# Layers 1 to 3 of a gated cross-attention decoder: the second token group's transposes and query products issued among the attention's leading tiles

## The chip, the cores and the metric

The kernel runs on one core of a Trainium2 chip. The metric is the device time of one execution in microseconds (us), median of the runs shown; a second number, the span, comes from a profiled execution and leaves out what lies before the first and after the last recorded instruction. The engines are named as in the profile: PE (TensorE matmul), PEld (its weight loads), DVE (VectorE), ACT (ScalarE), POOL (GpSimd), SP (SyncE, which issues most DMAs).

## What is computed

Four decoder layers act on a float32 stream x of 4 sequences of 256 tokens and 256 channels; the context has 64 tokens of 64 channels per sequence. Each layer adds a gated cross-attention and then a gated feed-forward part, each fed by a layer norm of x:

```python
x = x + tanh(g_xattn[0]) * L0_xattn(layernorm(x), ctx);  x = x + tanh(g_ffn[0]) * L0_ffn(layernorm(x))  # 16 experts, top 6
x = x + tanh(g_xattn[1]) * L1_xattn(layernorm(x), ctx);  x = x + tanh(g_ffn[1]) * L1_ffn(layernorm(x))  # ternary weights
x = x + tanh(g_xattn[2]) * L2_xattn(layernorm(x), ctx);  x = x + tanh(g_ffn[2]) * L2_ffn(layernorm(x))  # int8-like linear
x = x + tanh(g_xattn[3]) * L3_xattn(layernorm(x), ctx);  x = x + tanh(g_ffn[3]) * L3_ffn(layernorm(x))  # 8 experts, top 2
```

The attention of layer 1 has latent keys and values (16 heads of 128, folded by the kernel into weights that map x straight to a 64-wide latent query per head); those of layers 2 and 3 are plain 16-head attention with head size 16, a causal mask and a scale of 1/4:

```python
qp = q @ Wq.T;  k, v = split(latent_kv @ Wkv_expand.T)
attn = softmax(where(causal, q_h @ k_h.T / sqrt(16), lowest));  out = (attn @ v_h) @ Wout.T
```

## The kernel before

The 1024 tokens are 8 tiles of 128 (`NT`), in two groups of 4 tiles = 512 tokens (`NG`, `TH`). All of x stays in SBUF, one buffer per tile.

`layernorm(g)` (lines 374 to 398) takes the statistics of a group's four tiles on DVE (L379, L380), the square root on ACT (L382), and writes four normalised tiles `xn` on DVE (L394), or on ACT for layer 3 (L391). `transposed` (L400) turns them with 8 PE transposes (L406) into `xT`, through two PSUM tiles of the tag `mm` (4 buffers). `evacuate` (L128) copies out of PSUM, one call on ACT (L132) and the next on DVE (L134) in turn. `mm2` (L418, products at L421) makes one query product out of two matmuls over the 256 channels.

Each attention then goes over the 8 tiles in `in_flight` (L458): in round i it asks an optional generator `beside` for one step, makes the scores and exponentials of tile i, adds the output of tile i-3 to x (`gated_add`, L456), normalises the weights of tile i-1 (`weights`: sum L435 and reciprocal L436 on DVE, product L437 on POOL), and attends with tile i-2. Scores go into PSUM tiles `wide` (2 buffers). The row maximum and the subtraction are on DVE (layer 1: L427, L428; layers 2 and 3: L934, L936), the exponential on ACT (L429, L945). `attend` begins with 8 transposes of the weights (L451) and their two copies on ACT (L452); in layer 1 the products with the values follow (L656); in layers 2 and 3 the products L953, a copy on ACT (`ctxTok`, L962) and the output products (L965).

Ahead of the first tile of the attention, both groups' inputs are made:

- Layer 1 (`attention1`, L833): group 0's layer norm and transposes, its first 4 query products, group 1's layer norm and transposes, then the other 12 of the 16 query products (L842, 128 x 512 each), each copied by `evacuate` into the latent queries `qcT`. `latent_attend` (L610) also makes the values of a sequence (L623) every second tile, and its scores are L641.
- Layers 2 and 3 (`attention23`, L887): for both groups the layer norm, the transposes and two query products; then four scaled copies on ACT (L902) into separate tiles `qT`, which take the buffers of the tag `xT` (2 buffers). The scores are L923, with the mask added by L913 for every second tile.

In layer 2, `keyed` (L974) passes the making of layer 3's keys and values (`keys_values`: L860, L863, L875, L882) as `beside`, one step per round; layer 3 passes nothing.

A scheduler of the framework takes the program's order as a priority and decides the order in which each engine gets its instructions; on the chip each engine's queue is then followed in that order.

Of the kernel before, what the change touches and what calls it, by code (L numbers as in the profile page):

```python
# [16 lines left out]


# [1 line left out]

# [1 line left out]

# [6 lines left out]
F32 = mybir.dt.float32  # L29
# [8 lines left out]
P = 128  # L38
# [3 lines left out]
TH = 512  # L42
NG = T // TH
# [3 lines left out]
NP = NH // 2  # L47
# [34 lines left out]
def tile_flamingo(ctx: ExitStack, tc: tile.TileContext, a: dict, out: bass.AP):  # L82
    nc = tc.nc
# [316 lines left out]
    def transposed(tiles, dtype=F32):  # L400

        xT = sb.tile([P, 2, TH], dtype, tag="xT", name="xT", bufs=2)
        for c in range(2):
            ps = ps_mm()
            for i, n in enumerate(tiles):
                nc.tensor.transpose(ps[:, i * P : (i + 1) * P], n[:, c * P : (c + 1) * P], ident)  # L406
            evacuate(xT[:, c, :], ps)
        return xT
# [9 lines left out]
    def mm2(ps, w, xT):  # L418

        for c in range(2):  # L420
            nc.tensor.matmul(ps, w(c), xT[:, c, :], start=(c == 0), stop=(c == 1))  # L421
# [36 lines left out]
    def in_flight(scores, attend, gate, beside=iter(())):  # L458

        made, outs = {}, {}  # L460
        for i in range(NT + 3):
            next(beside, None)
            if i < NT:
                made[i] = scores(i)
            if i >= 3:
                gated_add(i - 3, outs.pop(i - 3)[:, :D], gate)
            if 1 <= i <= NT:
                weights(made[i - 1])
            if 2 <= i < NT + 2:
                outs[i - 2] = attend(i - 2, made.pop(i - 2))  # L470
# [136 lines left out]
        t = big[:, HALF:].rearrange("p (g r t) -> p g r t", g=NG, r=NP)  # L607
        return [t[:, g] for g in range(NG)]

    def latent_attend(qcT, wvo, gate, swapped=False):  # L610


        vos: dict = {}

        def values(b):

            v = region(("wqk", "weff")[b % 2], 2048, "vo").rearrange("p (q j o) -> p q j o", q=4, j=2)
            for r in range(2):
                pss = [ps_mm() for _ in range(2)]
                for a_ in range(2):  # L620
                    for j, ps in enumerate(pss):
                        rows = slice(j * DC, (j + 1) * DC)
                        nc.tensor.matmul(  # L623
                            ps[a_ * L : (a_ + 1) * L, :],
                            bd_k[rows, b, j * L : (j + 1) * L],
                            wvo[rows, 4 * r + a_ : 4 * r + a_ + 3 : 2, :],
                            start=True,
                            stop=True,
                        )
                for j, ps in enumerate(pss):  # L630
                    evacuate(v[:, 2 * r : 2 * r + 2, (1 - j) if swapped and b >= B // 2 else j, :], ps.rearrange("p (q o) -> p q o", q=2))
            vos[b] = v.rearrange("p q j o -> p (q j) o")

        def scores(t):
            g, i = divmod(t, TPG)
            if t % 2 == 0:
                values(t // 2)
            ps = ps_wide()
            for pr in range(NP):
                q, a_ = divmod(pr, 2)  # L640
                nc.tensor.matmul(  # L641
                    ps[:, q // 2, q % 2 * 256 : (q % 2 + 1) * 256].rearrange("p (j a l) -> p j a l", j=2, a=2)[:, :, a_, :],
                    qcT[g][:, pr, i * P : (i + 1) * P],
                    bd_k[:, t // 2, :],
                    start=True,
                    stop=True,
                )
            e = t4([P, NH, L], "attn")
            exponentials(e, ps.rearrange("p a (h l) -> p (a h) l", l=L))
            return e  # L650

        def attend(t, e):
            aT, vo = transposed_pairs(e), vos[t // 2]
            ps = ps_mm()
            for s in range(NP):
                nc.tensor.matmul(ps[:, :D], aT[:, s, :], vo[:, s, :], start=(s == 0), stop=(s == NP - 1))  # L656
            return ps

        in_flight(scores, attend, gate)

    def attention0(gate):

# [170 lines left out]
    def attention1(gate):  # L833
        weff, wvo = kept.pop("fold1")
        qcT = latents()
        xT = [transposed(layernorm(0))]
        for g in range(NG):
            for pr in range(NP):
                if g == 0 and pr == NP // 2:
                    xT.append(transposed(layernorm(1)))  # L840
                ps = ps_mm()
                mm2(ps, lambda c: weff[:, c, pr * P : (pr + 1) * P], xT[g])  # L842
                evacuate(qcT[g][:, pr, :], ps)
        latent_attend(qcT, wvo, gate)


    def keys_values(layer, kbd, vbd):
# [39 lines left out]
    def attention23(layer, gate, beside):  # L887
        kbd, vbd = kept.pop(layer)
        w = loaded[f"L{layer}"]
        w_q = w[:, :512].rearrange("p (c o) -> p c o", c=2)  # L890
        w_o = w[:, 512:1024].rearrange("p (c o) -> p c o", c=2)
        products, qT = [], []
        for g in range(NG):
            xT = transposed(layernorm(g, layer == 3))
            pss = [ps_mm() for _ in range(2)]
            for half, ps in enumerate(pss):
                mm2(ps, lambda c: w_q[:, c, half * P : (half + 1) * P], xT)
            products.append(pss)
        for pss in products:
            q = sb.tile([P, 2, TH], F32, tag="xT", name="qT", bufs=2)  # L900
            for half, ps in enumerate(pss):
                nc.scalar.mul(q[:, half, :], ps, 0.25)  # L902
            qT.append(q)

        def scores(t):


            g, i = divmod(t, TPG)
            ps = ps_wide()
            masked = t % 2 == 0  # L910
            if masked:
                for a in range(2):
                    nc.tensor.matmul(  # L913
                        ps[:, a, :].rearrange("p (h l) -> p h l", l=L),
                        ident16,
                        causal16.unsqueeze(1).to_broadcast([P, 8, L]),
                        start=True,
                        stop=False,
                    )
            for half in range(2):  # L920
                for a in range(2):
                    rows = slice(a * L, (a + 1) * L)
                    nc.tensor.matmul(  # L923
                        ps[:, a, half * D : (half + 1) * D],
                        qT[g][rows, half, i * P : (i + 1) * P],
                        kbd[rows, half, t // 2].rearrange("p i l -> p (i l)"),
                        start=not masked,
                        stop=(half == 1 or not masked),
                    )

            e = t4([P, NH, L], "attn")
            src = ps.rearrange("p a (h l) -> p (a h) l", l=L)
            mx = small([P, NH], "mx")
            nc.vector.tensor_reduce(mx, src, AX.X, ALU.max)  # L934
            for a in range(2):
                nc.vector.tensor_tensor(  # L936
                    e.rearrange("p (f a i) l -> p a f i l", f=2, a=2)[:, a],
                    ps[:, a, :].rearrange("p (f i l) -> p f i l", f=2, l=L),
                    mx[:, a * 8 : (a + 1) * 8]
                    .rearrange("p (f i) -> p f i", f=2)  # L940
                    .unsqueeze(3)
                    .to_broadcast([P, 2, 4, L]),
                    ALU.subtract,
                )
            nc.scalar.activation(e, e, AF.Exp)  # L945
            return e

        def attend(t, e):
            aT = transposed_pairs(e)
            ps = ps_mm()  # L950
            for pr in range(NP):
                half, r = divmod(pr, 4)
                nc.tensor.matmul(  # L953
                    ps[r * 32 : (r + 1) * 32, half * P : (half + 1) * P],
                    vbd[:, t // 2, pr].rearrange("p j d -> p (j d)"),
                    aT[:, pr, :],
                    start=True,
                    stop=True,
                    tile_position=(0, r * 32),
                )  # L960
            cT = sb.tile([P, 2 * P], F32, tag="xn", name="ctxTok", bufs=6)
            nc.scalar.copy(cT, ps[:, : 2 * P])  # L962
            ps = ps_mm()
            for half in range(2):
                nc.tensor.matmul(  # L965
                    ps[:, :D], cT[:, half * P : (half + 1) * P], w_o[:, half, :], start=(half == 0), stop=(half == 1)
                )
            return ps

        in_flight(scores, attend, gate, beside)  # L970
        if layer == 3:
            used("L3")

# [826 lines left out]
```

## Time and profile before

| | |
|---|---|
| runs, us | 954.0, 962.89, 962.95; median 962.89 |
| the profiled execution | 967.09 us, span 965.3 us, mean granted PE clock 0.941 |
| busy of the span | PE 856.9 us (89%), PEld 555.5, DVE 509.9 (53%), POOL 345.7, ACT 286.8 |
| attention of layer 1, from group 0's first transpose | 478.9 us to about 575 us of the span |
| attention of layer 2, from group 0's first transpose | 637.3 us to about 705 us |
| attention of layer 3, from group 0's first transpose | 723.9 us to about 782 us |

How to read it: times are us from the start of the span. In the timeline a row has start, duration, engine, line, operation, written and read tiles with shapes, how many instructions were merged, and in brackets the idle time of the engine just before and what ended it. In the tables of stretches each engine has its busy time and count of instructions, PEclk is the clock that PE was granted, as a share of full speed, and then DMA share and rate. A 128 x 512 float32 product of one weight block stands as two rows of PE, so that the two matmuls of a query product are four rows.

### The profile page before, as it was taken

What the parts mean: (1) busy time and instruction counts of PE and PEld (TensorE: products, weight loads), DVE (VectorE), ACT (ScalarE), POOL (GpSimd) and SP (SyncE); (2) the same over time, 40 slices, a digit from 0 to 9 for tenths busy, and PEclk for the clock granted to TensorE, in tenths of its full rate; (3) what the DMA queues carried; (4) which work ended last, traced back from release to release, by engine and by line L of the source; (5) the groups of instructions that cost most, each with busy time, mean ns of one, the idle gap of its engine ahead of it and who ended that gap; (6) DMA issues with size and microseconds to landing.
All of it is one profiled execution on the core that took longest, in us unless ns stands there. A gap on an engine that the chain in (4) does not pass through costs nothing.

```text
span 965.3 us, 12724 instructions
## 1 busy us (share of the span) xinstructions
PE 856.9 (89%) x4467; PEld 555.5 (58%) x4467; DVE 509.9 (53%) x1299; ACT 286.8 (30%) x559; POOL 345.7 (36%) x262
## 2 busy tenths in 40 slices
PE   6999999999999999986199986997867889999994
PEld 4444336876667876764046872754544556666662
DVE  4566648748624444571427755867776856222220
ACT  2122014433112322322113445415534441122221
POOL 1454543110146787786001323402311302144421
PEclk9999999999779999998599999986988999999998
DMA  9201157000256666655640000360000012122223
GB/s 364 79 21 34 61 160 200 22 22 9 84 129 158 125 141 150 121 82 63 186 174 1 1 1 0 111 227 1 1 22 1 1 44 54 43 45 45 39 23 66
DMA packets 38762, 75.15 MB, mean 78 GB/s; under 512 B 6240, under 2 KB 26706, under 8 KB 37322
## 3 DMA queue, kind: packets, MB, share of 16 engines
q1 hardware_dynamic: 23562, 52.01, 16.0%
q0 software_dynamic: 14496, 20.47, 13.1%
q10 hardware_dynamic: 640, 1.84, 0.5%
q8 instruction: 39, 0.64, 0.3%
q14 instruction: 25, 0.20, 0.1%
HBM read 58.73 MB, written 16.61 MB: 78 GB/s over the span
## 4 chain that ended last, share of the span: by engine, by line
PE 31%; DVE 10%; issue 4%; ACT 3%; POOL 2%; DMA 0%; POOLq 0%; ACTq 0%; DVEq 0%
PE wide L1226 7%; PE mm L421 5%; PE mm L1250 3%; PE wide L1436 2%; PE mm L451 2%; PE mm L656 2%; PE mm L965 2%; PE wide L923 1%; PE mm L1457 1%; DVE mx L934 1%; DVE attn L936 1%; PE mm L1637 1%; PE mm L1241 1%; DVE big L1483 1%; POOL h L1482 1%
## 5 line engine op out<-in xcount | busy, mean ns | idle before, releaser
L437 POOL TENSOR_TENSOR attn<-attn,sm 128x1024 f32<-128x1024 f32 x32 | 60.9, 1903 | 212.5 <-DVE sm L436 192.5
L1235 DVE SCALAR_TENSOR_TENSOR blk<-wide,weight,blk 128x176 f32<-128x176 f32 (+1 forms) x75 | 37.0, 493 | 135.3 <-ACT blk L1234 121.2
L1262 POOL DMA_INDIRECT sums<-ring,big x55 | 88.1, 1601 | 33.6 <-issue 10.2
L421 PE MATMUL wide<-xT,big 128*128 128x512 f32 x192 | 86.7, 600 | 0.3 <-ACT big L556 0.3
L683 DVE TENSOR_TENSOR rope<-wide,big 128x512 f32<-128x512 f32 x96 | 59.6, 683 | 47.7 <-PE wide L421 46.6
L1174 POOL DMA_INDIRECT xs<-xd,big x55 | 54.9, 999 | 63.3 <-DMA sums<-x 35.6
L1215 PE MATMUL wide<-big,blk 128*128 x220 | 77.1, 472 | 0.0
L1226 PE MATMUL wide<-big,blk 128*128 x160 | 72.2, 593 | 0.5 <-DVE blk L1187 0.5
L1234 ACT ACTIVATE blk<-wide 128x176 f32<-128x176 f32 (+1 forms) x75 | 29.4, 392 | 122.3 <-PE wide L1226 60.2
L421 PEld LDWEIGHTS wide<-xT,big 128*128 128x128 f32 x192 | 35.0, 190 | 46.7 <-issue 40.5
L656 PE MATMUL mm<-vo,attnT 128*128 128x256 f32 x256 | 59.5, 386 | 0.9 <-ACT attnT L452 0.9
L1250 PE MATMUL mm<-big,blk 88*128 x220 | 57.4, 383 | 0.6 <-ACT blk L1243 0.5
L406 PE MATMUL mm<-ident,xn 128*128 128x128 f32 x112 | 19.4, 320 | 41.6 <-DVE xn L394 35.5
L656 PEld LDWEIGHTS mm<-vo,attnT 128*128 128x128 f32 x256 | 48.0, 193 | 9.1 <-ACT attnT L452 3.1
L456 DVE SCALAR_TENSOR_TENSOR x<-mm,tg,x 128x256 f32<-128x256 f32 x48 | 22.9, 478 | 54.9 <-PE mm L656 17.3
L1250 PEld LDWEIGHTS mm<-big,blk 88*128 88x128 f32 x220 | 41.9, 192 | 16.5 <-ACT blk L1243 1.5
L452 ACT COPY attnT<-mm 128x512 f32<-128x512 f32 x64 | 35.0, 588 | 54.6 <-PE mm L451 54.3
L1215 PEld LDWEIGHTS wide<-big,blk 128*128 128x128 f32 x220 | 40.6, 196 | 13.2 <-issue 1.3
L451 PE MATMUL mm<-ident,attn 128*128 128x128 f32 x256 | 38.0, 297 | 9.9 <-POOL attn L437 9.9
L435 DVE TENSOR_REDUCE sm<-attn 128x16 f32<-128x1024 f32 x32 | 38.8, 1212 | 14.9 <-ACT attn L429 12.4
L1174 POOL DMA_INDIRECT xs<-xd,scratch x20 | 19.5, 976 | 74.6 <-PE mm L1186 53.9
L1262 POOL DMA_INDIRECT sums<-ring,scratch x20 | 31.5, 1573 | 39.3 <-ACT ring L1261 16.8
(321 smaller groups left out, 1698.6 us busy)
## 6 DMA issues: line engine op xcount, KB each, us to landing
big<-in_L_w_gate_up SPq DMA_DIRECT2D x8, 1024.0 KB
big<-in_L_w SPq DMA_DIRECT2D x4, 1408.0 KB
big<-in_L_w_down SPq DMA_DIRECT2D x8, 512.0 KB
w_L_qk<-in_L_qk SPq DMA_DIRECT2D x4, 896.0 KB
big<-in_L_w SPq DMA_DIRECT2D x4, 704.0 KB
big<-in_L_wo SPq DMA_DIRECT2D x1, 2048.0 KB
xd<-xn SPq DMA_DIRECT2D x16, 128.0 KB
sums<-x SPq DMA_DIRECT2D x16, 128.0 KB
```

What stands on the lines that cost most here:

```text
L421: nc.tensor.matmul(ps, w(c), xT[:, c, :], start=(c == 0), stop=(c == 1))
L435: nc.vector.tensor_reduce(sm, e, AX.X, ALU.add)
L437: nc.gpsimd.tensor_tensor(e, e, sm.unsqueeze(2).to_broadcast([P, groups, n]), ALU.mult)
L451: nc.tensor.transpose(ps[:, i * P : (i + 1) * P], ev[:, pr * P : (pr + 1) * P], ident)
L656: nc.tensor.matmul(ps[:, :D], aT[:, s, :], vo[:, s, :], start=(s == 0), stop=(s == NP - 1))
L683: nc.vector.tensor_tensor(m[:, s, :].rearrange("q (b t) -> q b t", t=S), ps[:, s, :].rearrange("q (b t) -> q b t", t=S), table, ALU.mult,)
L1174: nc.gpsimd.indirect_dma_start(out=xs, out_offset=None, in_=self.xd, in_offset=bass.IndirectOffsetOnAxis(ap=self.gather[:, b : b + 1].bitc ...
L1215: nc.tensor.matmul(ps[:, 0, : 2 * n], st[:, c * P : (c + 1) * P], self.w[:, bass.ds(r + c * 2 * n, 2 * n)], start=False, stop=(c == 1),)
L1226: nc.tensor.matmul(ps[:, k, :n], st[:, c * P : (c + 1) * P], self.w[:, bass.ds(r + (2 * c + k) * n, n)], start=(c == 0), stop=(c == 1),)
L1235: nc.vector.scalar_tensor_tensor(s, lin, self.weight.pop(b), s, ALU.mult, ALU.mult)
L1250: nc.tensor.matmul(ps[:, :D], hT[:, j * P : (j + 1) * P], self.w[: self.chunk, bass.ds(r + j * D, D)], start=(j == 0), stop=(j == self.n - 1),
L1262: nc.gpsimd.indirect_dma_start(out=self.sums[b % len(self.sums)], out_offset=bass.IndirectOffsetOnAxis(ap=self.scatter[:, b : b + 1].bitca ...
```

## The change

In layers 1 to 3 only group 0's layer norm, transposes and queries are made ahead of the attention. Those of group 1 become a generator, `queries(1)`, that `in_flight` steps through by `beside`: in round 0 its layer norm; in layer 1 the transposes and 4 query products in round 1 and 4 more in round 2; in layers 2 and 3 the transposes in round 1 and the two products with their scaled copies in round 2. The scores of group 1 begin with tile 4. In layer 2 the generator for layer 3's keys and values is stepped along with it. In layers 2 and 3 the queries are written over the inputs `xT` in place of tiles of their own. `latent_attend` gets the parameter `beside`, and hands it on.

```diff
-    def latent_attend(qcT, wvo, gate, swapped=False):
+    def latent_attend(qcT, wvo, gate, swapped=False, beside=iter(())):
...
-        in_flight(scores, attend, gate)
+        in_flight(scores, attend, gate, beside)
...
     def attention1(gate):
         weff, wvo = kept.pop("fold1")
         qcT = latents()
-        xT = [transposed(layernorm(0))]
-        for g in range(NG):
+        def queries(g):
+
+            xn = layernorm(g)
+            yield
+            xT = transposed(xn)
             for pr in range(NP):
-                if g == 0 and pr == NP // 2:
-                    xT.append(transposed(layernorm(1)))
                 ps = ps_mm()
-                mm2(ps, lambda c: weff[:, c, pr * P : (pr + 1) * P], xT[g])
+                mm2(ps, lambda c: weff[:, c, pr * P : (pr + 1) * P], xT)
                 evacuate(qcT[g][:, pr, :], ps)
-        latent_attend(qcT, wvo, gate)
+                if pr % 4 == 3:
+                    yield
+
+        for _ in queries(0):
+            pass
+        latent_attend(qcT, wvo, gate, beside=queries(1))
...
     def attention23(layer, gate, beside):
...
-        products, qT = [], []
-        for g in range(NG):
-            xT = transposed(layernorm(g, layer == 3))
+        qT = []
+
+        def queries(g):
+
+            xn = layernorm(g, layer == 3)
+            yield
+            xT = transposed(xn)
+            yield
             pss = [ps_mm() for _ in range(2)]
             for half, ps in enumerate(pss):
                 mm2(ps, lambda c: w_q[:, c, half * P : (half + 1) * P], xT)
-            products.append(pss)
-        for pss in products:
-            q = sb.tile([P, 2, TH], F32, tag="xT", name="qT", bufs=2)
             for half, ps in enumerate(pss):
-                nc.scalar.mul(q[:, half, :], ps, 0.25)
-            qT.append(q)
+                nc.scalar.mul(xT[:, half, :], ps, 0.25)
+            qT.append(xT)
+
+        for _ in queries(0):
+            pass
...
-        in_flight(scores, attend, gate, beside)
+        in_flight(scores, attend, gate, zip_longest(queries(1), beside))
```

## The prediction

> **What bounds the kernel now.** I read the page's busy line first, then the tables of stretches for the three attentions, then the timeline around their first tiles. By the page PE is the bound:
>
> ```profile
> PE 856.9 (89%) x4467; PEld 555.5 (58%) x4467; DVE 509.9 (53%) x1299; ACT 286.8 (30%) x559; POOL 345.7 (36%) x262
> ```
>
> But 89% is a mean over stages, and a PE at half clock counts as busy. The stretches show who waits where (us, PE busy, PEld, DVE, ACT, POOL, PEclk, DMA share, GB/s):
>
> ```profile
> 489.00:510.60 21.60, 21.60 (x58) 9.81 (x56) 4.84 (x7) 4.10 (x7) 0.00 (x0) 1.00 0.23 82
> 520.00:525.00 5.00, 2.93 (x22) 2.72 (x21) 5.00 (x6) 1.05 (x2) 1.90 (x1) 0.91 0.00 0
> ...
> 648.00:652.00 4.00, 4.00 (x22) 2.40 (x21) 0.62 (x1) 1.29 (x3) 0.00 (x0) 1.00 0.00 0
> 656.00:660.00 4.00, 1.14 (x9) 0.77 (x9) 4.00 (x7) 2.53 (x6) 0.45 (x1) 1.00 0.00 0
> 668.00:672.00 4.00, 4.00 (x13) 2.37 (x13) 1.72 (x3) 1.24 (x4) 1.90 (x1) 0.50 0.00 0
> 684.00:688.00 4.00, 4.00 (x38) 2.84 (x38) 3.90 (x8) 2.49 (x6) 0.97 (x2) 1.00 0.02 4
> ```
>
> Ahead of each attention PE is full and DVE nearly idle (rows 1 and 3: query products). In the leading tiles it is the reverse: DVE full, PE idle (rows 2 and 4). Then in layer 2 PE looks full but has half its clock, with DVE waiting (row 5); only in row 6 do both run. Layer 1's later tiles are bound by PE, those of layers 2 and 3 by DVE. The timeline names the waits: the maxima wait for the first scores, PE for POOL's first weights, and the first addition for the first output.
>
> ```profile
> 523.92 1.84 PE L451 MATMUL mm<-ident,attn 128*128 128x128 f32 x8 [2.07 <-POOL attn L437]
> ...
> 645.29 1.04 PE L406 MATMUL mm<-ident,xn 128*128 128x128 f32 x8
> 646.57 3.70 PE L421 MATMUL mm<-xT,w_L 128*128 128x512 f32 x8 [0.24 <-ACT xT L132]
> 651.38 1.23 DVE L934 TENSOR_REDUCE mx<-wide 128x16 f32<-128x1024 f32 x1 [4.32 <-PE wide L923]
> 661.50 1.97 PE L451 MATMUL mm<-ident,attn 128*128 128x128 f32 x8 [0.89 <-POOL attn L437]
> 668.83 0.48 DVE L456 SCALAR_TENSOR_TENSOR x<-mm,tg,x 128x256 f32<-128x256 f32 x1 [4.18 <-PE mm L965]
> ...
> 734.81 1.22 DVE L934 TENSOR_REDUCE mx<-wide 128x16 f32<-128x1024 f32 x1 [4.32 <-PE wide L923]
> 751.10 0.48 DVE L456 SCALAR_TENSOR_TENSOR x<-mm,tg,x 128x256 f32<-128x256 f32 x1 [3.00 <-PE mm L965]
> ```
>
> **The change, part by part.** I read the order in which the changed program's instructions stand on each engine. SP's and POOL's are the same, so no DMA and no POOL product passes another. DVE's and PE's instructions are the same in number; ACT gets two more table loads, in layer 2. Group 1's statistics and normalised tiles stay ahead of tile 0's maximum; what moves behind tile 0's scores is 8 transposes, two copies and the query products.
>
> *Layer 1.* Moved: 8 transposes and 8 products (1.04 + 32 rows of 0.43 = 14.8 us of PE), with ten copies on ACT and DVE. PE runs all of it before and after, so only its idle time can go: 2.07 at 523.92, and the half clock that follows that gap (PEclk 0.56 from 524.5 to 527.9: 3.4 x 0.44 = 1.5). Together 3.6. Given back: group 1's second xT copy (0.69) stands on DVE behind tile 0's maximum (1.23), so its first product waits 1.92 after the scores, of which transposes and one score (1.04 + 0.24) cover 1.3: 0.6 to 0.8 idle. DVE's later copies stand behind a subtraction or a sum (1.2 each), but a product takes PE 1.72 and four PSUM buffers are there, so PE need not stop. Bounds: 0 to -3.6. I take **-2.5**, 0.4 under the difference, for the new hand-overs.
>
> *Layer 2, start.* PE ends group 0's queries at 645.4; two scaled copies (1.09) follow at once, not behind group 1's transposes. They can't begin earlier, as they overwrite xT, which the last product reads. So the first scores end at about 647.8 against 651.4: 4.74 of PE work leaves the front, 1.1 of ACT becomes bare: -3.6. From there DVE has, in the changed order, maximum 1.23, xT copy 0.69, subtraction 1.29, maximum 1.21, subtraction 1.29, sum 1.21, reciprocal 0.24: 7.2, so POOL's first product starts at 655.0 against 659.55 (before, tile 2's maximum and half its subtraction stood in between): -4.5. Beside this PE does group 1's products until about 654, then tile 2's scores (0.61 + 1.14) until 656; ACT's copies of group 1 fit between exponentials of 1.06.
>
> *Layer 2, clock.* Before, PE was busy only 0.68 of the 3.4 us ahead of 661.0 and had half its clock from 661.0 to 678.0. The additions of tiles 0 to 3 come at 668.83, 677.19, 683.51, 688.49: steps of 8.36, 6.32 and 4.98, and layer 3, at full clock, makes 3.95, 4.78, 4.23 and 5.26 (751.10 to 769.32). With the query products in the gap PE waits about 1 us for POOL, not 4. At full clock transposes, copies, exponential of tile 2 and outputs bring the first addition to about 663.7 (-5.1), and two steps at layer 3's slowest, 5.26, in place of 14.68, give -4.2 more. Here a page speaks against me: the Trainium skill, "TensorE: Matmul & The Clock Gate", section "Part 4: PE-mode transpose", says transposes don't count as PE being busy; so the 1.04 of transposes hold nothing and the 3.70 of products, with the scores, must do it. Its Part 1 makes a drop cheap: one busy window of about 3.4 us brings the clock back, so 1.7 us lost. The trace shows 17 us at half clock with PE busy throughout, some 6 us in those steps. By the page this part would be worth about -1.5; by the rows -4.2, which I take.
>
> *Layer 2, end.* The scheduler now puts ffn2's square root ahead of tile 7's exponential, so the table is loaded twice more. "ScalarE: Activation LUTs", section "What ACT_TABLE_LOAD costs", gives 2.66 us a switch, drain included: 5.3. Here a load takes 1.28 and the exponential starts 1.29 after the load does (layer 1, 556.53 and 557.82): 2.6. Tile 7's weights were ready 2.4 before its transposes (697.8 against 700.2), and one load falls under DVE; I charge 0.3, between 0 and 2.6. Layer 2: -5.1 - 4.2 + 0.3 = **-9**; with the clock lost as before, about **-4.5**.
>
> *Layer 3.* PE ends group 0's products at 728.9. Two scaled copies (1.2) interleave with group 1's last normalisation on ACT (0.5): first scores' end at 731.3 against 734.8, -3.5. DVE's chain of 7.2 puts POOL's first product at 738.5 against 742.4. Then DVE has another 7.6 (two sums, two maxima, two subtractions, a reciprocal) until 746.1; tile 0's output is due at about 745.5 even at half clock, so the addition comes at 746.1 against 751.10: DVE's wait of 3.00 goes. Later tiles keep DVE's pace. Bounds: -3 (only the earlier start, less the copy) to -5. I take **-4.5**.
>
> Sum: -2.5 - 9 - 4.5 = -16. The profiled execution gives 967.1 - 16 = 951.1. It stood 4.2 above the median of the runs shown; from that median I forecast 962.9 - 16 = **947 us**.
>
> **Rivals.** *Clock lost again in layer 2.* The windows are free-running, and tile 2's scores (1.75) with uncounted transposes may fill one too thinly: before, windows with PE busy 0.68 and 1.13 lost the clock, one with 1.67 kept it, and one with 1.90, part of it transposes, lost it. Gain -2.5 - 4.5 - 4.5 = -11.5, less where layer 3 gives -3: **952**. *Eaten by the queues.* DVE is already full in rows 2 and 4, and the copies are new work there: if each of layer 1's five DVE copies holds PE by half of a 1.2 us operation (3), layer 2's and 3's chains by one more such operation each (2.4), and the clock is lost, 6 remain: **957**. Against it: the copies were made before as well, and PE has other work queued. *Slower.* One mechanism: after thinner PE work in layer 2 the clock stays at half through all its tiles. A tile then costs 8.36 in place of about 5: eight tiles lose 27, of which before already lost some 6; against gains of 11.5 the time is **972**. It decides once half clock lasts about 27 us longer than the 17 before (0.4 us lost per us). For it: five fully busy windows did not bring the clock back. Against it: layer 3, with the same operations, came back after two. That the change doesn't reorder is excluded by the orders.
>
> **How the numbers follow.** Forecast 0.50, clock lost again 0.25, eaten 0.16, slower 0.09. A measurement of this kernel tells about 1% from no change, 9.6 us. Faster by more: the forecast and 0.18 of the second, 0.68. Within: 0.07 of the second and the third, 0.23. Slower: 0.09, the fourth. The low end is layer 1's and 3's bounds and a further 5.26 step, about -20, and 4 for runs near the fastest before: 938. The high end takes in the third: 959. That leaves out the slower case and some of the edges.
>
> **What would show it.** Right: in layer 1 no wait of 2 us before L451's first transposes and no half clock near it; in layers 2 and 3 L934 first some 3.5 us after group 0's products, with no wait of 4 us for L923; L456's first addition about 26 us (not 31) after group 0's first transposes in layer 2, 22 (not 27) in layer 3; PEclk 1.00 through layer 2's tiles; stages shorter by 2.5, 9 and 4.5. Wrong: PE idle within group 1's products, DVE copies with PE waiting on them, or PEclk 0.50 for more than a few us.

## The result, and the profile after

The changed kernel takes 949.25 us (median of 947.2, 948.66, 949.85 and 951.8) against 962.92 for the kernel before (954.0, 962.89, 962.95 and a later execution of 966.99; the profiled one took 967.09); the ratio estimated from these runs is 0.9878 with a 95% interval of 0.9847 to 0.991, while the medians alone give 0.9858. The interval leaves out 1: the change makes the kernel about 1.2% faster. The forecast was 947. The profiled execution took 947.2 us, with a span of 945.4 and a mean PE clock of 0.959. The lines of the changed program stand one lower than before up to L457, and further down below: L421 is now L422, L451 L452, L456 L457, L902 L911, L923 L935, L934 L946, L936 L948, L945 L957, L962 L974, L965 L977.

The busy line of the page after; nearly all work is the same, with two more instructions on ACT:

```profile
PE 844.9 (89%) x4464; PEld 547.3 (58%) x4467; DVE 514.0 (54%) x1299; ACT 288.7 (31%) x561; POOL 344.5 (36%) x262
```

The table of stretches after (us, PE busy, PEld, DVE, ACT, POOL, PEclk, DMA share, GB/s). The first row is the place in layer 1 where PE had a hole. Then layer 2 in three pieces: from group 0's first transposes to tile 0's maximum, to the first addition, to the last one. The last two rows are layer 3, before and behind its first addition.

```profile
521.00:526.00 5.00, 5.00 (x37) 4.72 (x36) 3.95 (x7) 1.69 (x3) 1.91 (x1) 1.00 0.00 0
629.92:639.02 9.10, 8.52 (x26) 4.05 (x26) 4.01 (x12) 2.23 (x5) 0.70 (x1) 0.71 0.84 288
639.02:655.09 16.07, 15.18 (x87) 8.66 (x88) 14.13 (x18) 10.81 (x20) 3.75 (x2) 1.00 0.01 2
655.09:689.32 34.23, 29.49 (x232) 18.13 (x230) 25.10 (x50) 20.40 (x38) 11.58 (x8) 0.95 0.00 1
708.79:730.22 21.43, 19.45 (x109) 11.10 (x107) 16.17 (x30) 11.61 (x19) 3.80 (x2) 1.00 0.00 1
730.22:760.36 30.14, 25.55 (x222) 16.34 (x221) 23.58 (x50) 15.79 (x28) 11.41 (x6) 1.00 0.04 14
```

In row 3 PE (15.18 of 16.07) and DVE (14.13) are busy together, at full clock; this is the piece where they had taken turns. Its counterpart before, between L934 at 651.38 and L456 at 668.83:

```profile
651.38:668.83 17.45, 12.42 (x67) 7.29 (x64) 13.20 (x18) 10.12 (x17) 3.80 (x2) 0.76 0.01 2
668.83:704.33 35.50, 32.13 (x234) 19.36 (x234) 23.39 (x49) 19.11 (x38) 11.60 (x8) 0.88 0.00 1
```

The timeline after, at the places that the prediction named: L452's first transposes in layers 1 and 2, the first maximum and the first addition of layer 2, and the same three of layer 3.

```profile
517.84 1.04 PE L452 MATMUL mm<-ident,attn 128*128 128x128 f32 x8
...
639.02 1.22 DVE L946 TENSOR_REDUCE mx<-wide 128x16 f32<-128x1024 f32 x1 [4.28 <-PE wide L935]
648.24 1.09 PE L452 MATMUL mm<-ident,attn 128*128 128x128 f32 x8 [0.89 <-POOL attn L438]
655.09 0.47 DVE L457 SCALAR_TENSOR_TENSOR x<-mm,tg,x 128x256 f32<-128x256 f32 x1
...
715.56 1.22 DVE L946 TENSOR_REDUCE mx<-wide 128x16 f32<-128x1024 f32 x1 [4.00 <-PE wide L935]
724.57 1.09 PE L452 MATMUL mm<-ident,attn 128*128 128x128 f32 x8 [1.75 <-POOL attn L438]
730.22 0.47 DVE L457 SCALAR_TENSOR_TENSOR x<-mm,tg,x 128x256 f32<-128x256 f32 x1
```

The wait of 2.07 us in layer 1 is gone (no bracket), the first transposes of layer 2 take 1.09 and not 1.97, and the first additions no longer wait. DVE still waits 4.28 and 4.00 us for the first scores, since the layer norm of both groups is still ahead of them; but the wait ends earlier.

Where the time went, between the two profiles (us; a stage runs from group 0's first transposes to the start of the last addition):

| stretch | before | after | difference |
|---|---|---|---|
| up to layer 1's stage | 478.90 | 475.51 | -3.4 |
| layer 1's stage | 96.27 | 93.14 | -3.1 |
| to layer 2's stage | 62.08 | 61.27 | -0.8 |
| layer 2's stage | 67.08 | 59.40 | -7.7 |
| to layer 3's stage | 19.58 | 19.47 | -0.1 |
| layer 3's stage | 57.95 | 51.57 | -6.4 |
| to the end of the span | 183.44 | 185.04 | +1.6 |

The first row lies ahead of any changed instruction. Before, 23.9 us of half clock stood there around 255 to 279; after, 3.4 us around 270. So a single pair of profiles says too much: 3.4 us of its 19.9 arose before the change could act, and the medians differ by 13.7. What differs between executions of one program, above all where PE's clock is halved and for how long, is called a draw from here on. The last row may be such a draw too: after has one half-clock stretch of 3.4 us just behind layer 3's stage (768 to 772), before had it inside the stage. The experiments had to tell how much of layer 2's 7.7 is a draw as well.

### The profile page after: what moved, and what is told of

Same layout as the page of the kernel before. It is cut to its first block, busy times and chain, and to the rows that moved or that the text cites. A ratio compares the mean times of both kernels' runs of the same rounds, so it can differ in the third digit from the quotient of the medians.

```text
span 945.4 us, 12712 instructions
## 1 busy us (share of the span) xinstructions
PE 844.9 (89%) x4464; PEld 547.3 (58%) x4467; DVE 514.0 (54%) x1299; ACT 288.7 (31%) x561; POOL 344.5 (36%) x262
## 5 line engine op out<-in xcount | busy, mean ns | idle before, releaser
L422 PE MATMUL wide<-xT,big 128*128 128x512 f32 x192 | 88.3, 610 | 0.3 <-ACT big L557 0.3
L422 PEld LDWEIGHTS wide<-xT,big 128*128 128x128 f32 x192 | 35.8, 193 | 47.6 <-issue 41.3
L407 PE MATMUL mm<-ident,xn 128*128 128x128 f32 x112 | 19.9, 322 | 41.5 <-DVE xn L395 35.4
L1227 PEld LDWEIGHTS wide<-big,blk 128*128 128x128 f32 x220 | 40.7, 196 | 13.3 <-issue 1.2
L436 DVE TENSOR_REDUCE sm<-attn 128x16 f32<-128x1024 f32 x32 | 38.8, 1213 | 16.3 <-ACT attn L430 13.7
L1238 PEld LDWEIGHTS wide<-big,blk 128*128 128x128 f32 x160 | 28.8, 190 | 28.9 <-issue 28.2
L407 PEld LDWEIGHTS mm<-ident,xn 128*128 128x128 f32 x112 | 15.1, 162 | 47.2 <-ACT rstd L383 27.6
```

The costliest lines, as they stand in the source:

```text
L436: nc.vector.tensor_reduce(sm, e, AX.X, ALU.add)
L1227: nc.tensor.matmul(ps[:, 0, : 2 * n], st[:, c * P : (c + 1) * P], self.w[:, bass.ds(r + c * 2 * n, 2 * n)], start=False, stop=(c == 1),)
L1238: nc.tensor.matmul(ps[:, k, :n], st[:, c * P : (c + 1) * P], self.w[:, bass.ds(r + (2 * c + k) * n, n)], start=(c == 0), stop=(c == 1),)
```

## The experiments

Stages, in us, of every profile. "Half clock" is what lay between layer 2's first maximum and its last addition, in us, from the granted clock in stretches of 1 us; it comes in multiples of about 3.4. The three pieces of layer 2 are those of the stretches above.

| run | layer 1 | layer 2 | its pieces | half clock | layer 3 |
|---|---|---|---|---|---|
| before | 96.27 | 67.08 | 14.13, 17.45, 35.50 | 17.1 | 57.95 |
| e5 before again | 96.62 | 62.80 | 14.42, 16.97, 31.41 | 6.8 | 57.17 |
| e1 layer 1 only | 92.72 | 63.37 | 14.80, 17.17, 31.40 | 6.8 | 57.21 |
| e3 thirteen products | 96.60 | 65.33 | 14.41, 14.71, 36.21 | 6.8 | 57.08 |
| e9 ten products | 96.28 | 59.66 | 14.10, 14.15, 31.41 | 0 | 57.95 |
| after | 93.14 | 59.40 | 9.10, 16.07, 34.23 | 3.4 | 51.57 |
| e6 after again | 93.10 | 59.40 | 9.05, 16.07, 34.28 | 3.4 | 51.58 |
| e11 after, timed | 92.47 | 61.29 | 10.06, 16.07, 35.16 | 6.8 | 51.57 |
| e2 layers 2 and 3 only | 96.83 | 59.71 | 9.87, 16.07, 33.77 | 3.4 | 53.17 |
| e4 products only | 92.32 | 61.14 | 10.52, 15.46, 35.16 | 6.8 | 55.89 |
| e8 copies on ACT | 93.35 | 59.43 | 9.25, 16.07, 34.11 | 3.4 | 52.49 |
| e7 root later | 92.18 | 57.73 | 9.90, 16.07, 31.76 | 0 | 51.58 |
| e10 root later, timed | 91.83 | 57.65 | 9.82, 16.07, 31.76 | 0 | 51.58 |

### e1: layer 1 alone

`attention1` and `latent_attend` as after, `attention23` as before:

```diff
-        xT = [transposed(layernorm(0))]
...
-        latent_attend(qcT, wvo, gate)
+        latent_attend(qcT, wvo, gate, beside=queries(1))
```

> Only layer 1's order is changed; layers 2 and 3 stand as before. Stages are read from L451/L452's first transposes to the last addition L456/L457 (before 96.27, 67.08, 57.95; after 93.14, 59.40, 51.57). Theory (the order fills PE's idle lead, each layer by itself): layer 1 at 93 to 93.5 us, layer 2 at 66 to 68, layer 3 at 57 to 58.5, the whole about 3 us under the kernel before (ratio 0.997), which single times cannot tell from its own spread. Rival (layer 1's gain was the clock's luck: its half-clock stretch near 525 fell elsewhere in the other profile): layer 1 at 95 to 96.5 again, or 93 with a half clock of 3.4 us merely displaced. Second rival (layer 1's order shifts the phase of the clock's windows for layer 2 and this made layer 2's gain): layer 2 at about 60 here too.

Measured: ratio 0.9966 (0.9946 to 0.9986), 956.37 us against 960.35. Layer 1 took 92.72 and layer 3 stayed at 57.21, so each layer gains by itself. Layer 2, whose instructions stand as before, took 63.37 and not 67.08, with 6.8 us of half clock in place of 17.1: between the theory's 66 to 68 and the second rival's 60, and the first sign that 67.08 was no fixed cost. That layer 1's new order made it is excluded by e5, where nothing is changed.

### e2: layers 2 and 3 alone

`attention1` as before, `attention23` as after:

```diff
-        in_flight(scores, attend, gate, beside)
+        in_flight(scores, attend, gate, zip_longest(queries(1), beside))
```

> Layers 2 and 3 in the new order, layer 1 as before. Theory: layer 1 at 96 to 96.5 with its wait of about 2 us before the first transposes, layer 2 at 59 to 60.5, layer 3 at 51 to 52; the whole some 13 to 14 us under before (ratio 0.986). Rival (layer 2's gain needs layer 1's shift, by the phase of the clock's windows): layer 2 at 62 to 67 with a half-clock stretch among its first four tiles, layer 3 unchanged at 51 to 52; the whole -7 to -10.

Measured: ratio 0.9917 (0.9886 to 0.9947), 951.53 us: some -8 by the ratio, not the -13 to -14 of the theory, which took before's longest draw for its cost. The stages came as the theory had them for layers 1 and 2 (96.83, 59.71); layer 3 took 53.17, since a half clock of 3.4 us fell on its first tiles. With e1 the two halves make -0.34% and -0.83%, together -1.2%, which is the whole change: they add up.

### e3: thirteen unused products, before's order

```diff
+            if t == 2:
+                idle = ps_mm()
+                for _ in range(13):
+                    nc.tensor.matmul(
+                        idle.rearrange("p (h l) -> p h l", l=L),
+                        ident16,
+                        causal16.unsqueeze(1).to_broadcast([P, 8, L]),
+                        start=True,
+                        stop=True,
+                    )
```

> The order before, and in layers 2 and 3 thirteen unused products of 128x512 in bf16 (about 0.3 us each, 4 us in all) behind tile 2's scores, where PE was idle: work added only to keep PE busy. Theory (the start is set by the order, the clock is an addition to it): in layer 2 the half clock of 17 us is gone, POOL's first product and so the first addition stay where they were but for the transposes and outputs at full clock (30 to 31 us after group 0's first transposes, not 25), two steps shorten by about 4, of which the later tiles give 1 to 3 back since DVE has no lead then: 62 to 65 us in place of 67.08; layer 3, which had full clock already, stays at 57.5 to 58.5. Rival (layer 2's gain was nearly all clock): layer 2 at 59 to 60.5. Rival (half clock doesn't come from the idle gap): half clock is there again, and layer 2 stays at 66 to 68.

Measured: ratio 0.9998 (0.998 to 1.0015). Layer 2 took 65.33, with its first addition at 29.12 us. Among layer 2's tiles there was no half clock until 686.1, so it can be kept off by keeping PE busy. The rest is no clean test: with so many products the scheduler moved sums and maxima on DVE, and put the next stage's square root ahead of tile 7's exponential, with two more table loads. The last piece grew to 36.21. It was repeated with fewer products as e9.

### e4: only the products moved

In layers 2 and 3 group 1's transposes stay ahead of tile 0's scores:

```diff
             xn = layernorm(g, layer == 3)
-            yield
             xT = transposed(xn)
             yield
+            yield
```

> The new order, but in layers 2 and 3 group 1's eight transposes and two copies stay ahead of tile 0's scores; only its query products go behind tile 1's scores. Theory (DVE's chain from tile 0's maximum sets the start): scores end 1.04 us later, but the 0.69 us copy leaves the chain behind the maximum and is made while DVE is idle: layers 2 and 3 at 59.4 and 51.6 with +0.3 to +0.6 each. Rival (PE's work ahead of the first scores sets it): +1.0 to +1.7 each. Rival (the copy behind the maximum is what costs): -0.5 or less each.

Measured: ratio 0.9907 (0.9874 to 0.9941). Layer 2 took 61.14, next to the 61.29 of the changed kernel under the same half clock (e11). So the place of the eight transposes is worth nothing that shows; the 3.70 us of products is what had to move. In layer 3 the stage reached its first weights' transposes in 15.56 us (709.54 to 725.10), 0.2 less than after (15.78), and then ran 10.3 us at half clock, for 55.89. All the loss of 4.3 lies behind that point. None of the three theories had this: with the products moved, the clock can still be lost in the lead, as e2 shows with the full change (3.4 us). Whether e4's order makes a longer loss likelier, one profile can't tell.

### e5 and e6: both kernels once more

> The kernel before, once more, to see how much of layer 2 is the draw of the clock and not the order. In its first profile layer 2 had half clock for 17.1 us from 661 and took 67.08; with only layer 1 changed it had 6.8 us from 656 and took 63.37. Theory (the same instructions draw different windows): layer 2 between 63 and 67 with a half clock of 7 to 17 us somewhere in its first five tiles, longer where it lasts longer; layer 1 at 96.3 and layer 3 at 57 to 58 as before. Rival (17 us belongs to this program): layer 2 at 67 again.

> The changed kernel once more. Theory: layers 1, 2 and 3 at 92.5 to 93.5, 59.4 to 60 and 51.5 to 53.5, with no half clock in layer 2's tiles until the last ones; layer 3 may draw one stretch of 3.4 us, worth 1.6. Rival (its clock was luck as well): half clock among layer 2's first tiles and 61 us or more.

Measured: 960.47 and 948.28 us (one execution each). The table of stretches of e5, in the three pieces of layer 2:

```profile
635.17:649.59 14.42, 13.66 (x43) 6.94 (x44) 4.82 (x13) 3.64 (x8) 0.75 (x1) 0.76 0.62 206
649.59:666.56 16.97, 11.94 (x67) 7.13 (x64) 13.20 (x17) 10.12 (x17) 3.80 (x2) 0.80 0.01 2
666.56:697.97 31.41, 28.03 (x234) 17.06 (x234) 23.30 (x50) 19.02 (x38) 11.60 (x8) 1.00 0.00 1
```

The same program as before, with the half clock over after 6.8 us, makes its last piece in 31.41, not 35.50. So 4.1 us of layer 2's 7.7 belong to the one execution that the prediction was read from. Against e5 the changed order gains 3.4 there. The changed kernel's stages came again to 0.1 us in e6 (93.10, 59.40, 51.58).

### e7: the square root held back

```diff
-        nc.scalar.activation(rstd, mv[:, :, 1], AF.Sqrt, bias=eps)
+        kept["root"] = nc.scalar.activation(rstd, mv[:, :, 1], AF.Sqrt, bias=eps)
...
-            nc.scalar.activation(e, e, AF.Exp)
+            kept["exp"] = nc.scalar.activation(e, e, AF.Exp)
...
             xn = layernorm(g, True)
+            if g == 0:
+                behind(kept["root"], kept["exp"])
```

> The changed kernel with the square root of the next stage held behind tile 7's exponential in layer 2, so that the two extra table loads (1.28 us each) are gone. In the profile of after tile 7's exponential waits 1.3 us for its table (differences 676.6 to 677.9) and its sum, its product on POOL and its transposes follow it. Theory (tile 7's chain ends the stage): layer 2 at 58.0 to 58.4 in place of 59.4, -1.0 to -1.4. The prediction's 0.3 (the loads are hidden): 59.0 to 59.4. Rival (both loads count, and the square root costs nothing later): 56.8 to 57. The whole differs by less than single times can tell.

`behind` keeps the first instruction from being issued ahead of the second. Measured: 947.71 us (four runs, 943.89 to 948.74), ratio 0.9883 (0.9849 to 0.9916). Layer 2 took 57.73, 1.7 less than after, between the theory and the rival that both loads count. The timeline after shows ACT and PE around the loads:

```profile
673.30 1.28 ACT L383 ACT_TABLE_LOAD   x1
676.61 1.28 ACT L957 ACT_TABLE_LOAD   x1 [0.55 <-DVE attn L948]
677.91 1.06 ACT L957 ACTIVATE attn<-attn 128x1024 f32<-128x1024 f32 x1
678.87 0.35 ACT L974 COPY ctxTok<-mm 128x256 f32<-128x256 f32 x1
...
679.28 1.87 PE L977 MATMUL mm<-w_L,ctxTok 128*128 128x256 f32 x4 [2.73 <-ACT ctxTok L974]
680.94 1.91 PE L452 MATMUL mm<-ident,attn 128*128 128x128 f32 x8
```

And in e10, the same program as e7, at the same place:

```profile
676.11 1.06 ACT L957 ACTIVATE attn<-attn 128x1024 f32<-128x1024 f32 x1 [0.56 <-DVE attn L948]
677.07 0.35 ACT L974 COPY ctxTok<-mm 128x256 f32<-128x256 f32 x1
...
677.48 1.13 PE L977 MATMUL mm<-w_L,ctxTok 128*128 128x256 f32 x4 [1.46 <-ACT ctxTok L974]
678.67 1.09 PE L452 MATMUL mm<-ident,attn 128*128 128x128 f32 x8
```

The exponential waits for its table, the copy `ctxTok` of another tile stands behind it in ACT's queue, and PE waits 2.73 for that copy in place of 1.46. Then PE's products take 1.87, not 1.13: the clock has gone. The tables of stretches, after first and then e10:

```profile
676.50:679.90 3.40, 0.67 (x6) 0.54 (x3) 3.40 (x10) 2.60 (x3) 1.90 (x1) 0.94 0.00 0
679.90:683.30 3.40, 3.35 (x19) 2.38 (x18) 1.84 (x5) 0.99 (x2) 1.90 (x1) 0.55 0.00 0
```

```profile
676.00:679.40 3.40, 1.89 (x15) 1.41 (x12) 3.07 (x12) 2.90 (x4) 1.90 (x1) 1.00 0.00 0
679.40:682.80 3.40, 2.55 (x28) 1.63 (x27) 2.22 (x4) 1.45 (x3) 1.90 (x1) 1.00 0.00 0
```

PE was busy 0.67 of 3.4 us and lost the clock; busy 1.89, it kept it. How much of the 1.7 us is the wait and how much the clock was not separated. All six profiles of the changed order with the loads (after, e2, e4, e6, e8, e11) have a half clock at this place, of 3.4 or 6.8 us; neither without them (e7, e10) has one.

### e8: group 1's copies on ACT

```diff
-            evacuate(xT[:, c, :], ps)
+            (nc.scalar.copy if scalar else evacuate)(xT[:, c, :], ps)
...
-            xT = transposed(xn)
+            xT = transposed(xn, scalar=g == 1)
```

> The changed kernel with both copies of group 1's inputs on ACT in layers 2 and 3, so that DVE's chain from tile 0's maximum to POOL's first product loses its 0.69 us copy. Theory (that chain sets the start): the first addition 0.6 to 0.7 earlier in both layers, stages 58.7 and 50.9. Rival (ACT is late instead: the exponential of tile 0 stands behind the second copy, 0.59): first addition unchanged to +0.5, stages 59.4 to 60 and 51.6 to 52. Rival (given back by DVE's pace in later tiles): first addition earlier, the stage's end unchanged.

Measured: 948.56 us, ratio 0.9881 (0.9862 to 0.99). The theory fell: the first addition of layer 2 came at 25.32 us and not at 24.5, that of layer 3 at 22.16 against 21.43, and layer 3 took 52.49. But ACT was not late, as the first rival had it. In layer 3 tile 0's exponential starts 9.40 us after the first transposes, where after has 9.82, and POOL's first product 13.35 after them in place of 13.82: the chain did get shorter. What came later is tile 3's maximum, which stands ahead of the first addition on DVE: 18.69 us after the transposes, and not 17.96. The exponentials and these maxima, in after and then in e8:

```profile
718.61 1.06 ACT L957 ACTIVATE attn<-attn 128x1024 f32<-128x1024 f32 x1 [0.92 <-DVE attn L948]
...
726.75 1.22 DVE L946 TENSOR_REDUCE mx<-wide 128x16 f32<-128x1024 f32 x1 [0.79 <-PE wide L935]
```

```profile
719.47 1.06 ACT L957 ACTIVATE attn<-attn 128x1024 f32<-128x1024 f32 x1
...
728.76 1.23 DVE L946 TENSOR_REDUCE mx<-wide 128x16 f32<-128x1024 f32 x1 [1.75 <-PE wide L935]
```

The scheduler had put part of tile 3's scores on PE behind tile 0's products with the values. So in layer 3 the first addition is set by the scores of tile 3, not by the chain to POOL alone.

### e9: ten unused products, in layer 2 alone

The edit of e3 with `if t == 2 and layer == 2` and `range(10)`. The orders on DVE and ACT are those of before.

> The order before, and in layer 2 alone ten unused products of 128x512 in bf16 behind tile 2's scores; the orders on DVE and ACT are those of before to the instruction, and there are no more table loads. Before's own draws of layer 2: 67.08 with 17.1 us of half clock, 63.37 and 62.80 with 6.8. Theory (half clock is paid in its length, about 0.4 us per us, and the rest is order): no half clock among the tiles, first addition 28.5 to 29.5 after group 0's first transposes, layer 2 at 60.0 to 61.5, still above the changed order at 57.7 to 59.4. Rival (nearly all of layer 2's gain is clock): 59.4 or less. Rival (DVE and ACT set the pace once the start is past, so a start that is 2.5 earlier is given back): 62.5 to 63.

Measured: 957.4 us (one execution). Layer 2 took 59.66, a little below the theory's 60.0 to 61.5, and 0.3 above the changed kernel. The last two of its three pieces, as stretches:

```profile
649.00:663.15 14.15, 11.41 (x77) 6.21 (x75) 13.20 (x18) 10.02 (x17) 3.80 (x2) 1.00 0.01 2
663.15:694.56 31.41, 28.03 (x234) 17.05 (x234) 23.30 (x50) 19.02 (x38) 11.59 (x8) 1.00 0.00 1
```

PE in the hole, in the timelines of e9 (the first two rows) and of e5 (the third):

```profile
653.21 2.12 PE L934 MATMUL mm<-causal,ident 128*128 128x512 bf16 x9
659.12 1.09 PE L451 MATMUL mm<-ident,attn 128*128 128x128 f32 x8 [0.89 <-POOL attn L437]
```

```profile
659.71 1.97 PE L451 MATMUL mm<-ident,attn 128*128 128x128 f32 x8 [0.89 <-POOL attn L437]
```

Nine of the ten products stand in the hole (the tenth ran at 650.6): 2.1 us of work that nobody reads keep the clock, and the middle piece falls from 16.97 (e5) to 14.15, by 2.8; the last piece is the same, 31.41. So the usual half clock of 6.8 us costs 2.8, or 0.4 per us, and what the changed order has in layer 2 over a before that keeps its clock is small: 59.66 to 59.40 with the table loads, to 57.7 without. The 0.3 is within the draw of the first piece, where half clock took 6.3 us in e9 and 5.2 in after.

### e10 and e11: timed side by side

> The changed kernel with the square root held behind tile 7's exponential, timed more often and beside the changed kernel on the same chip: its layer 2 was 57.73 against 59.40. Theory: 1.7 us under the changed kernel in the median (ratio to before 0.9865 against 0.988). Rival (what is gained there is waited for in the next stage): the same time as the changed kernel within 0.5 us, and the stretch from layer 2's last addition to layer 3's first transposes longer than 19.5 by what layer 2 is shorter.

> The changed kernel, timed beside the one with the later square root. From the parts measured: layer 1 -3.8, layer 2 -3.4 to -4 against before's shorter draws, layer 3 -5.6: -13, so a ratio to before of 0.9865; with before's longer draws of the clock up to -17. If the first profile's -20 were the rule, 0.980.

Measured: e10 944.12 us (943.26 to 946.07), ratio 0.9852 (0.981 to 0.9895); e11 947.54 us (944.95 to 948.7), ratio 0.9882 (0.9839 to 0.9924). The intervals of the ratios overlap, but five of e10's six runs lie below all six of e11, the medians differ by 3.4, and the stage repeats (57.73, 57.65 against 59.40, 59.40, 61.29). In the earlier timing the same program as e10 stood closer: e7's median of 947.71 beside 948.28 for e6's one execution. So the stage's 1.7 us or more is shown, and the size of the gain in the whole is not settled. From layer 2's last addition to layer 3's first transposes e10 takes 19.36 us, as after (19.47), so the gain is not given back. The changed kernel with the later square root has the lowest median of the versions run here. The change itself stands at -1.2%, some 11.5 us; the sum of the stages against e5 is -12.5.

## Why the prediction was right, and where its steps were not

**Layer 1: -2.5 forecast, -3.1 in the pair of profiles, -3.9 between the means of all profiles of either order (96.5 and 92.6).** The mechanism is as told: the wait of 2.07 is gone and with it the half clock behind it. The step that was too large is the charge for new hand-overs, "0.6 to 0.8 idle" at group 1's first product. After:

```profile
497.94 0.59 ACT L133 COPY xT<-mm 128x512 f32<-128x512 f32 x1 [1.86 <-PE mm L407]
498.58 0.30 PEld L422 LDWEIGHTS mm<-xT,weff 128*128 128x128 f32 x2 [0.25 <-ACT xT L133]
498.60 0.68 DVE L135 COPY xT<-mm 128x512 f32<-128x512 f32 x1
```

The second copy is indeed behind tile 0's maximum on DVE (498.60), but the product begins at 498.58, released by ACT's copy of the other half of xT, and PE has no gap there. The gain is a little above the upper bound of 3.6. Each profile has half clock at the beginning of this stage, 4.2 to 5.3 us of it in the old order and 3.4 to 6.5 in the new; PE is busy there throughout (4.18 of 4.22 us before, 5.99 of 6.03 after), so half of it is lost. With that half taken off, all five stages of the old order stand at 94.2 and all eight of the new at 90.1: 4.0 us, of which the wait is 2.07 and the half clock behind it, 3.4 us at 0.50, is 1.7.

**Layer 2, head: tile 0's maximum 3.6 earlier forecast, 5.0 in the pair.** The step that failed is "They can't begin earlier, as they overwrite xT, which the last product reads". The timeline after, PE's products and ACT's scaled copies:

```profile
632.67 4.91 PE L422 MATMUL mm<-xT,w_L 128*128 128x512 f32 x8 [0.46 <-ACT xT L133]
637.51 1.46 PE L935 MATMUL wide<-kbd,xT 64*128 64x256 f32 x8
...
636.82 0.60 ACT L911 ACTIVATE xT<-mm 128x512 f32<-128x512 f32 x1 [4.01 <-PE mm L422]
637.62 0.60 ACT L911 ACTIVATE xT<-mm 128x512 f32<-128x512 f32 x1 [0.20 <-PE mm L422]
```

The first copy starts at 636.82, while the products run until 637.58. It writes only channel half 0 of xT, and the last rows read half 1. The first score follows at once, so the copies cost next to nothing: the means of the first piece are 14.4 before and 9.6 after (e4 left out). This piece too has 5.1 to 6.8 us of half clock in every profile; with half of that taken off, before, e5 and e9 have 11.0 and after, e6 and e10 6.5. So 4.5 of the 4.74 us left the front, not 3.6.

**Layer 2, chain to the first product on POOL: right.** 7.2 forecast from DVE's durations; 7.27 measured (639.02 to 646.29). The first addition came 25.17 us after the first transposes and not 31.58: -6.4 for -5.1, and the 1.3 more is the head's. DVE's wait of 4 us for the first scores, whose absence was to be a sign of being right, stayed (4.28): it did not get shorter, it ended earlier.

**Layer 2, later tiles: -4.2 + 0.3 forecast, -1.3 in the pair.** Two terms were off. The -4.2 for two slow steps was there, since the steps after the first addition are 4.43 and 6.25 where they were 8.36 and 6.32; but it was a property of one execution, not of the kernel: before makes this piece in 31.4 us in e1, e5 and e9. And "I charge 0.3" for the two table loads was an eighth of their price. They hold ACT while tile 7 needs it, PE starves behind ACT's queue and loses its clock: 34.23 against 31.76 with the root held back, 2.5 us, just under the upper bound of 2.6. Together: against before's usual draw (e5, 62.80) layer 2 gains 3.4 and not 9, and nearly all of that is the clock, since e9 gains 3.1 in the old order. The earlier start is spent again in the middle piece and on the table loads.

**The clock, page against row.** For one order of instructions the half clock of layer 2's lead lasted 17.1 us in before and 6.8 in e1 and e5, while that of layer 1 lasted 3.4. By the Trainium skill, "TensorE: Matmul & The Clock Gate", Part 1, one busy window brings the clock back. In e5 and in layer 1 it came back after the first stretch of 3.41 us with PE busy throughout; in before not after the first three such, but after the fourth. Before, from the start of half clock:

```profile
660.62:664.03 3.41, 2.53 (x10) 2.07 (x10) 3.41 (x6) 1.52 (x3) 2.36 (x2) 0.50 0.02 5
664.03:677.69 13.66, 13.66 (x64) 7.61 (x62) 5.38 (x10) 3.53 (x8) 4.17 (x3) 0.50 0.00 1
```

So here the measurement contradicts the page, but 17 us did not come again and was no cost of the program. In each of the thirteen profiles half clock begins and ends on one grid of 3.41 us, whose phase against the program differs between executions; that this makes the draw is likely, but was not tested. Between 100 and 930 us, no stretch of that grid with PE busy under 1.5 us kept full clock. Above that the busy time does not decide: full clock was kept after 1.52 us (after, up to 389.38) and lost after 1.74 (e2, up to 729.38). That transposes don't count as busy, which the prediction took from the page, no run isolates.

**Readings to put right.** Before's half clock starts at 660.62, not 661.0, and PE was busy 1.06 us and not 0.68 in the 3.41 ahead of it; four of the five stretches that followed were fully busy, not five. The two slow steps hold 8.9 us of half clock (668.83 to 677.69), not some 6. The sign that L934 would come "some 3.5 us after" group 0's products does not follow from the prediction's own times, 645.4 and 647.8; it came 1.4 after them (637.58 to 639.02).

**Layer 3: -4.5 forecast, -6.4 in the pair, -5.6 against e5.** Head -4.1 (10.90 to 6.77) for -3.5, again since the copies cost less than charged; first addition 21.43 us after the first transposes, 22 forecast. "At full clock" is right for the steps that the prediction names (751.10 to 769.32), but not for the lead: before has half clock there in every profile (6.8 us from 742.5 here), after has none, e2 and e4 do. Behind the head the stage is 1.5 us shorter than in e5, 2.0 of it up to the first addition with 0.5 given back later. Half clock of 6.8 us at 0.4 per us would be 2.7, an estimate from e9, so those 2.0 may all be clock; no run fills layer 3's hole alone, and this stays open.

**The sum.** Forecast -16; measured -13.7 by the medians of the first set, -11.3 to -11.7 by the ratios. The pair of profiles has -17.2 in the three stages. The prediction took its -16 from a profiled execution 4.2 above the median, then subtracted it from the median: the 4.1 us that the long half clock cost lie in that difference and could not be saved twice. That it ended 2 us from the measured time is in part because layer 1 and the heads of layers 2 and 3 gave more than forecast (1.5, 0.9 and 0.6 us), and in part luck: the median of three runs that it started from, 962.9, lies 2.5 above the 960.35 of the 38 runs timed beside e1. From there -16 would have given 944.

**The rivals.** The clock was not lost again in layer 2's lead in any of the eight profiles of the changed order, where the middle piece stands at 16.07 to the last digit in seven of them (e4 has 15.46). In layer 3 it was lost in two of eight (e2, e4), for +1.6 and +4.3. Eaten by the queues: the middle piece is 1.9 longer than before's at full clock (16.07 against 14.15), so new work does stand in DVE's and PE's lead, but the head gives 4.5. Slower: the clock never stayed at half through layer 2's tiles; 6.8 us, at the end, is the longest there.

## What to carry to other kernels

Work that waits ahead of a pipeline's first tile, on an engine that then idles in the lead, is worth moving into the lead; here 4.1 to 4.5 of 4.7 us were gained at the front. How much of that reaches the end depends on what bounds the later tiles: in layer 2 little more than the clock. Before forecasting from one profile, see whether it lies above the median and which stage holds the surplus: a saving that is the surplus itself can't be taken from the median. Read from the order what the scheduler moves along: two table loads on an engine that is 31% busy cost 2.5 us, because another engine's work was queued behind them. And a clock that is lost in a hole can be worth more than the hole.

## What the runs showed of the hardware that was not expected

Unused work can be worth time: 2.1 us of products in a hole of PE shortened layer 2 by 3.1 us against e5, 2.8 of them in the piece with the hole. And half clock begins while PE is not idle but thin: it was lost with PE busy 0.67 us of 3.4 in after, and 1.06 in before.

A DVE operation on 128x4 elements, 0.14 us in before, took 1.80 in e10, and ended together with a POOL product that had begun ahead of it. DVE's rows of before and of e10, and POOL's of e10:

```profile
698.01 0.14 DVE L387 SCALAR_TENSOR_TENSOR shift<-mv,rstd 128x4 f32<-128x4 f32 x1
```

```profile
679.56 1.80 DVE L388 SCALAR_TENSOR_TENSOR shift<-mv,rstd 128x4 f32<-128x4 f32 x1
...
679.44 1.90 POOL L438 TENSOR_TENSOR attn<-attn,sm 128x1024 f32<-128x1024 f32 x1 [0.82 <-DVE rstd L384]
```

After has the same 1.80 at 677.35, ahead of tile 7's sum. A sum on DVE beside such a product keeps its 1.22. The Trainium skill, "Advanced Engine Details and Errata", Mode Summary, notes that DVE's second SBUF port is shared with GpSimd, and that DVE instructions of the two-port kind and GpSimd's block each other. The shift reads two SBUF tensors (mv and rstd), the sum one. But the number of tensors is not all: an operation on one of 128x4 (`xs`) took 1.48 us in after, from 691.03, and ended with a POOL operation as well (690.14 to 692.48). No run isolates the port.
